# A talking-heads attention with a soft mixture of experts: a pair's first block mixed on four 64x64 tiles of TensorE, in an order of TensorE that is written out

## The chip, the cores and the metric

The kernel runs on one core of one Trainium2 chip. The metric is the device time of one execution in microseconds (us); before the change its median over 3 runs is 9190.56 us (9187.51 to 9199.91). The profile comes from one further execution, which took 9193.65 us.

## What is computed

Four sequences (batches) of 2048 tokens with 256 features pass through an attention layer and an expert layer, each with a residual and a layer norm. All data are float32. What matters here is the attention, which mixes its 16 heads twice:

```
logits = einsum('bhid,bhjd->bhij', q, k) * SCALE        # 16 heads of 16 features
logits = einsum('bhij,gh->bgij', logits, Wpre)          # heads mixed before the softmax
attn   = softmax(logits, axis=-1)
attn   = einsum('bhij,gh->bgij', attn, Wpost)           # and mixed again after it
out    = einsum('bhij,bhjd->bhid', attn, v)             # then Wout, residual, layer norm
```

The expert layer normalises the tokens and the columns of `mu`, forms slot weights from their products, and runs 16 small experts.

## The kernel before

For each of the 4 batches `qkv` projects and rotates q and k, `attention` does the above, and `moe` the expert layer. `attention` goes over 128 **pairs**. A pair `n` is two **blocks** (x = 0, 1) of 8 tokens; a block's 8 tokens times 16 heads fill the 128 partitions. The 2048 keys are taken in two halves (j = 0, 1) of 1024. For each pair:

- `raw_banks(n, c)` (L351, matmul at L366) forms q times k for all heads, 16 matmuls of 32x32 weights and 512 columns for each of c = 0, 1, into four PSUM banks (tiles `s`). Four copies, by VectorE (`V`, L529) or ScalarE (`S_`, L532), take them to the tile `raw`.
- `raw_rows(n)` (L376, L388) moves `raw` by eight DMAs of 256 KB on SyncE's queue into four tiles `rows`, one for each (j, x), with (token, head) on the partitions.
- `logits(n, j)` (L390, L406) mixes the heads with `Wpre`, again by 32x32 matmuls, into two two-bank PSUM tiles `l`, one for each x.
- `top` (L418, L421) takes the row maximum on VectorE, `expo` (L426, L430) the exponential with its sum on ScalarE, back into `rows`.
- `shares` (L436) and `weights` (L451) join the two halves of the softmax in a chain of tiny operations: VectorE, GpSimd, ScalarE, GpSimd twice, VectorE, GpSimd twice. The last one (L458) multiplies `Wpost`, laid out block-diagonally over the 8 tokens (`wblk_sb`, 128x128), with the softmax factors: tile `w`.
- `mix(n, x, j)` (L468, L478) multiplies 8 stretches of 128 keys of `rows`, as weights, with `w` as moving operand: 8 matmuls of 128x128 with 128 columns, into two PSUM banks (tiles `t`), which are copied to `aT` (keys on partitions) by VectorE and ScalarE.
- `values(grp, hf)` (L490, L498) multiplies with v: 64 matmuls of 128x32 weights and 64 columns for each pair, and every eighth pair `finish` (L516, L522) applies `Wout`.

The code of iteration n works on three pairs: `logits`, `top`, `expo` of pair n; `raw_banks` and `raw_rows` of pair n+2; `weights` and `mix` of pair n-1; and `values` of a group that is complete. `mix` in half j takes block x = j with both halves of its keys.

PSUM has eight banks: four for the two tiles `l` (pool `ps_l`), four (pool `ps_t`, tag `t`) that `raw_banks`, `mix`, `values` and `finish` take in turn, so each taking waits for what was taken four before it to be copied out. `raw` has two buffers, `rows` 10.

What sets the order: instructions that pass through `tc.keep_in_program_order` (`keep`) stay in the order of the code on their engine: the large copies, `top`, `expo` and the DMAs of `raw_rows`. All others, TensorE's matmuls among them, are placed by a scheduler as the program is built. It puts TensorE's work of a half as `logits`, `raw_banks`, `mix`, and `values` behind the `mix` of one half in two.

Of the kernel before, what the change touches and what calls it, by code (L numbers as in the profile page):

```python
# [16 lines left out]
P = 128  # L17
HEADS = 16
# [7 lines left out]
def kernel(  # L26
# [35 lines left out]
    ROWS = 10  # L62
# [3 lines left out]
    HT = NT // 2  # L66

# [25 lines left out]
    for i in range(IB):  # L93
        nc.scalar.dma_start(
            wblk_sb[i * HEADS : (i + 1) * HEADS, :, i], wpost.rearrange("(h g) -> h g", g=HEADS)
        )
    wout_sb = const.tile([P, KC, D], F32, tag="wout", name="wout_sb")
# [3 lines left out]
    mu_sb = work.tile([P, KC, ES], F32, tag="rows", name="mu_sb", bufs=ROWS)  # L101
    nc.scalar.dma_start(mu_sb, mu.rearrange("(c p) e -> p c e", p=P))
# [5 lines left out]
    ones = work.tile([P, P], F32, tag="k1", name="ones", bufs=6)  # L108
    nc.gpsimd.memset(ones, 1.0)
# [23 lines left out]

    sq = work.tile([P, KC, ES], F32, tag="rows", name="sq", bufs=ROWS)
    nc.vector.tensor_mul(sq, mu_sb, mu_sb)
    pn = ps_t.tile([P, 512], F32, tag="t", name="pn")
    for c in range(KC):
        nc.tensor.matmul(pn[:, :ES], ones, sq[:, c], start=(c == 0), stop=(c == KC - 1))
    rmu = work.tile([P, ES], F32, tag="k1", name="rmu", bufs=6)
    nc.scalar.activation(rmu, pn[:, :ES], AF.Sqrt)  # L140
    nc.vector.tensor_scalar_max(rmu, rmu, NORM_EPS)
    nc.vector.reciprocal(rmu, rmu)
    mun = const.tile([P, KC, ES], F32, tag="mun", name="mun")
    for c in range(KC):
        nc.vector.tensor_mul(mun[:, c], mu_sb[:, c], rmu)


# [13 lines left out]

    def k1(shape, name):
        return work.tile(shape, F32, tag="k1", name=name, bufs=6)
# [85 lines left out]
    def load_x(b, t, name):  # L249
        xt = work.tile([P, D], F32, tag="x", name=f"{name}_{b}_{t}", bufs=2)  # L250
        nc.sync.dma_start(xt, x[b, ts(t, P), :])
        return xt


    def qkv(b):
# [9 lines left out]
        def project(t):  # L265
            xt = load_x(b, t, "x")
# [3 lines left out]
            xT = k1([P, KC, P], f"xT_{b}_{t}")  # L270
# [49 lines left out]
    def attention(b, y, qT, kT, v):  # L320
        keep = tc.keep_in_program_order
        st = new_stats(f"a{b}")
# [4 lines left out]
        def pair_q(n):  # L327
# [4 lines left out]
            qb = k1([P, KC, 2, 4, 2, 2, 2], f"qb_{b}_{n}")  # L332
# [18 lines left out]
        def raw_banks(n, c, engs):  # L351
# [11 lines left out]
            for r in range(4):  # L363
                rows = slice(32 * r, 32 * (r + 1))
                for q in range(4):
                    nc.tensor.matmul(  # L366
# [7 lines left out]
            return [lambda r=r: engs[r](raw[:, 4 * c + r, :], prs[r]) for r in range(4)]  # L374
# [15 lines left out]
        def logits(n, j):  # L390
# [11 lines left out]
            for x in range(2):  # L402
                for h in range(2):
                    for q in range(4):
                        c = (q + 2 * x + h) % 4
                        nc.tensor.matmul(  # L406
# [29 lines left out]
        def shares(n):  # L436
# [4 lines left out]
            nc.vector.tensor_tensor(m, m2[:, :, 0:1], m2[:, :, 1:2], ALU.min)  # L441
            f = small.tile([P, 2, 2], F32, tag="f", name=f"f_{b}_{n}")
            nc.gpsimd.tensor_tensor(f, m.to_broadcast([P, 2, 2]), m2, ALU.subtract)  # L443
            nc.scalar.activation(f, f, AF.Exp)  # L444
# [6 lines left out]
        def weights(n):  # L451

            s = state[n]
            f, z = s["f"], s["z"]
            nc.vector.reciprocal(z, z)  # L455
            nc.gpsimd.tensor_tensor(f, f, z.to_broadcast([P, 2, 2]), ALU.mult)
            w = work.tile([P, 4, HEADS * IB], F32, tag="w", name=f"w_{b}_{n}", bufs=2)
            nc.gpsimd.tensor_tensor(  # L458
                w,
                wblk_sb.rearrange("p g i -> p (g i)").unsqueeze(1).to_broadcast([P, 4, HEADS * IB]),  # L460
                f.rearrange("p x j -> p (x j)").unsqueeze(2).to_broadcast([P, 4, HEADS * IB]),
                ALU.mult,
            )
            s["w"] = w
# [3 lines left out]
        def mix(n, x, j, engs):  # L468
# [6 lines left out]
            for r in range(2):  # L475
                pt = ps_t.tile([P, 4, P], F32, tag="t", name=f"t_{b}_{n}_{x}_{j}_{r}")
                for a in range(4):
                    nc.tensor.matmul(  # L478
                        pt[:, a, :], e[:, ts(4 * r + a, P)], s["w"][:, 2 * x + j, :],
                        start=True, stop=True,  # L480
                    )
                t0 = j * HT + 4 * r
                engs[r](
                    aT[grp][:, t0 : t0 + 4, :, ts(k, IB)],
                    pt.rearrange("p a (g i) -> p a g i", i=IB),
                )

        outT = {}

        def values(grp, hf):  # L490
# [4 lines left out]
            for t in range(NT):  # L495
                for c in range(4):
                    g0 = 2 * (4 * hf + c)
                    nc.tensor.matmul(  # L498
# [7 lines left out]
            if part == 0 and hf == 0:  # L506
                outT[it] = k1([P, KC, P], f"aoT_{b}_{it}")
            dst = outT[it][:, hf, ts(part, GI)]
            nc.vector.tensor_copy(dst, po[:, 0, :])  # L509
            nc.vector.copy_predicated(dst, odd, po[:, 1, :])  # L510
            if hf == 1:
                aT.pop(grp)
                if part == P // GI - 1:
                    finish(it)

        def finish(it):  # L516
            oT = outT.pop(it)
            xt = load_x(b, it, "xr")
            nc.gpsimd.tensor_add(xt, xt, bout_sb)
            pz = ps_t.tile([P, 512], F32, tag="t", name=f"pz_{b}_{it}")  # L520
            for c in range(KC):
                nc.tensor.matmul(  # L522
                    pz[:, :D], oT[:, c, :], wout_sb[:, c, :], start=(c == 0), stop=(c == KC - 1)
                )
            nc.vector.tensor_add(y[:, it, :], pz[:, :D], xt)
            norm_stats(y[:, it, :], it, st)
# [8 lines left out]
        nop = [lambda: None] * 4  # L535
        for n in range(2):
            for c in range(KC):
                for f in raw_banks(n, c, (V, S_, V, S_)):
                    f()
            raw_rows(n)  # L540
        for n in range(n_pairs + 3):
            cur, nxt, prv = n < n_pairs, n + 2 < n_pairs, 0 < n <= n_pairs

            grp, hf = divmod(n - per - 1, per)
            val = 0 <= grp < N // GI
            for j in range(2):
                if cur:
# [225 lines left out]
```

## Time and profile before

| | us |
|---|---|
| profiled execution | 9193.65 |
| its span (first to last instruction of the core) | 9191.9 |
| four attention stages (95 to 2159, 2385 to 4445, 4671 to 6742, 6969 to 9034) | 2064, 2060, 2071, 2065 |
| between and behind them (projection, experts) | 95, 226, 226, 227, 158 |
| TensorE busy with matmuls | 8249.7 |
| VectorE busy | 5541.1 |
| ScalarE busy | 4961.1 |
| GpSimd busy | 1845.8 |

In the profile PE is TensorE's matmuls, PEld its weight loads (which overlap them), DVE VectorE, ACT ScalarE, POOL GpSimd, SP SyncE. A group's line has the source line, the engine, the operation, the tile written and the tiles read, the shape and the count, then the busy time in all and the mean of one in ns. One float32 matmul of the code stands as two weight loads and two matmul records, called passes here (16384 matmuls at L478, 32768 records). A matmul's record reaches from its start to a modelled end, so records of one stream overlap, and the time that one takes of TensorE is the distance between starts.

### The profile page before, as it was taken

Reading aid. Unit: us, or ns where it says so; the run is one execution under the profiler, and the core shown is the slowest. Engines: PE = TensorE matmul, PEld = TensorE weight load, DVE = VectorE, ACT = ScalarE, POOL = GpSimd, SP = SyncE. Lnnn points to the kernel's source line nnn. Section 1 sums busy time; section 2 is a strip of 40 time slices with the busy share of each in tenths; the row PEclk is TensorE's granted clock in tenths of the full one; section 3 lists DMA queues with packets and bytes.
Section 4 is the critical chain, followed back from the end, with each engine's and each line's share of the span. In section 5 each row is a group of like instructions: output and inputs, shape, how many; then the busy total and the mean of one; then the engine's idle time right before and its main releaser. Section 6 shows DMA issues by size and latency. Waiting matters only on the chain. (4 is left out here: it accounts for less than half of the span.)

```text
span 9191.9 us, 373485 instructions
## 1 busy us (share of the span) xinstructions
PE 8249.7 (90%) x166484; PEld 6122.8 (67%) x166484; DVE 5541.1 (60%) x9074; ACT 4961.1 (54%) x9758; POOL 1845.8 (20%) x6481
## 2 busy tenths in 40 slices
PE   7999999997899999999689999999968999999996
PEld 4666776675576677676556676767755666776675
DVE  5666666665666666666466666666645666666664
ACT  3555555553455555555345555555534555555553
POOL 2221222111221122211122211221112221122211
PEclk9999999998999999999899999999989999999998
DMA  4555555552455555555145555555514555555551
GB/s 104 136 136 136 136 133 136 133 139 53 111 136 132 136 136 134 135 135 136 48 112 135 136 137 134 136 134 134 136 45 113 135 135 135 136 138 133 136 135 45
DMA packets 654551, 1140.00 MB, mean 124 GB/s; under 512 B 95760, under 2 KB 127120, under 8 KB 652944
## 3 DMA queue, kind: packets, MB, share of 16 engines
q1 hardware_dynamic: 616704, 1099.18, 49.7%
q8 instruction: 1309, 21.45, 1.0%
q10 hardware_dynamic: 36240, 16.93, 0.7%
q14 instruction: 298, 2.44, 0.1%
HBM read 33.71 MB, written 8.39 MB: 5 GB/s over the span
## 5 line engine op out<-in xcount | busy, mean ns | idle before, releaser
L478 PEld LDWEIGHTS t<-w,rows 128*128 128x128 f32 x32768 | 3760.5, 193 | 1352.9 <-ACT raw L532 753.0
L478 PE MATMUL t<-w,rows 128*128 128x128 f32 x32768 | 3945.4, 279 | 444.0 <-ACT raw L532 439.1
L421 DVE TENSOR_REDUCE m<-l 128x1 f32<-128x1024 f32 x2048 | 2497.0, 1220 | 970.2 <-PE l L406 970.2
L532 ACT COPY raw<-s 128x512 f32<-128x512 f32 x2552 | 1445.6, 590 | 2782.7 <-PE s L366 1646.9
L430 ACT ACTIVATE rows<-l,m 128x1024 f32<-128x1024 f32 x2048 | 2315.1, 1130 | 68.4 <-DVE m L421 60.8
L366 PE MATMUL s<-kT,qb 32*32 32x512 f32 x32768 | 1766.5, 606 | 72.3 <-issue 61.6
L529 DVE COPY aT<-t 128x512 f32<-128x512 f32 x2048 | 1396.6, 682 | 354.5 <-PE t L478 353.7
L532 ACT COPY aT<-t 128x512 f32<-128x512 f32 x2048 | 1219.5, 596 | 596.8 <-PE t L478 596.6
L406 PE MATMUL l<-rows,wmix_sb 32*32 32x512 f32 x32768 | 1413.8, 601 | 59.6 <-issue 35.1
L529 DVE COPY raw<-s 128x512 f32<-128x512 f32 x1544 | 1055.3, 684 | 194.6 <-PE s L366 163.3
L366 PEld LDWEIGHTS s<-kT,qb 32*32 32x32 f32 x32768 | 667.2, 103 | 738.1 <-issue 485.5
L498 PE MATMUL o<-aT,v 128*32 128x64 f32 x65536 | 1024.6, 220 | 17.8 <-issue 17.8
L498 PEld LDWEIGHTS o<-aT,v 128*32 128x32 f32 x65536 | 941.4, 110 | 80.1 <-issue 19.1
L343 POOL TENSOR_TENSOR qb<-qT,hmask 128x16 f32<-128x16 f32 (+3 forms) x3584 | 650.5, 221 | 1437.5 <-PE s L366 1437.5
L443 POOL TENSOR_TENSOR f<-m,m 128x4 f32<-128x4 f32 x512 | 102.8, 201 | 3850.3 <-DVE m L441 3850.3
L455 DVE RECIPROCAL z<-z 128x2 f32<-128x2 f32 x512 | 85.1, 166 | 860.8 <-POOL z L448 860.8
L458 POOL TENSOR_TENSOR w<-wblk_sb,f 128x512 f32<-128x512 f32 x512 | 533.5, 1042 | 40.1
L406 PEld LDWEIGHTS l<-rows,wmix_sb 32*32 32x32 f32 x32768 | 337.8, 103 | 301.6 <-issue 139.9
L509 DVE COPY aoT<-o 128x32 f32<-128x32 f32 x512 | 98.3, 192 | 673.9 <-PE o L498 673.9
L430 ACT ACTIVATION_READ_ACCUMULATOR rows<-l,m 128x1 f32 x2048 | 435.7, 213 | 0.0
L446 POOL TENSOR_TENSOR zf<-f,z 128x4 f32<-128x4 f32 x512 | 103.2, 202 | 762.1 <-ACT f L444 762.1
L301 POOL TENSOR_TENSOR s<-qk,wq 128x256 f32<-128x256 f32 x128 | 115.8, 924 | 497.4 <-DVE qk L285 484.7
(122 smaller groups left out, 2620.4 us busy)
## 6 DMA issues: line engine op xcount, KB each, us to landing
rows<-raw SPq DMA_DIRECT2D x4096, 256.0 KB
x<-in_x_dram SPq DMA_DIRECT2D x64, 128.0 KB
xr<-in_x_dram SPq DMA_DIRECT2D x64, 128.0 KB
out_dram<-qT SPq DMA_DIRECT2D x16, 512.0 KB
wm<-in_w_dram ACTq DMA_DIRECT2D x8, 512.0 KB
wm<-in_w_dram ACTq DMA_DIRECT2D x4, 1024.0 KB
wq<-in_wqkvT_dram ACTq DMA_DIRECT2D x4, 768.0 KB
wq<-in_bqkv_dram ACTq DMA_DIRECT2D x4, 384.0 KB
```

The lines of the kernel that those rows point to most:

```text
L301: nc.gpsimd.tensor_mul(s[:, :, a, :], qk[:, :, 1 - a, :], ss[a])
L343: nc.gpsimd.tensor_tensor(qb[:, :, g, s0:s1, :, :, x].rearrange("p c s i h -> p c (s i) h"), qT[:, t, :, i0:i1].unsqueeze(3).to_broadcast( ...
L366: nc.tensor.matmul(prs[r][32 * q : 32 * (q + 1), :], qb[rows, c, q % 2].rearrange("p s i h x -> p (s i h x)"), kT[rows, c, ts(q, QN)], sta ...
L406: nc.tensor.matmul(pls[x][32 * c : 32 * (c + 1), ts(h, 512)], wmix_sb[32 * q : 32 * (q + 1), :], raws[n][j][x][32 * q : 32 * (q + 1), ts(h ...
L421: nc.vector.tensor_reduce(s["m2"][:, x, j : j + 1], s["l", j][x], AX.X, ALU.max, negate=True)
L430: nc.scalar.activation(s["e", j][x], s["l", j][x], AF.Exp, bias=s["m2"][:, x, j : j + 1], accum_out=s["z2"][:, x, j : j + 1],)
L446: nc.gpsimd.tensor_tensor(zf, f, z2, ALU.mult)
L458: nc.gpsimd.tensor_tensor(w, wblk_sb.rearrange("p g i -> p (g i)").unsqueeze(1).to_broadcast([P, 4, HEADS * IB]), f.rearrange("p x j -> p ...
L478: nc.tensor.matmul(pt[:, a, :], e[:, ts(4 * r + a, P)], s["w"][:, 2 * x + j, :], start=True, stop=True,)
L498: nc.tensor.matmul(po[32 * c : 32 * (c + 1)].rearrange("p a i -> p (a i)"), v[:, t, g0 * HD : (g0 + 2) * HD], at[:, t, g0 : g0 + 2, :].rea ...
L529: keep(nc.vector.tensor_copy(dst, src))
L532: keep(nc.scalar.copy(dst, src))
```

## The change

1. TensorE's matmuls in `attention` pass through `keep`, and the loop is rewritten: `values` first, then in each half `raw_banks`, `logits`, `mix` of both blocks of pair n-1 with that half of the keys. `values` comes one iteration later (n - per - 2 in place of n - per - 1), and the copies stand in a fixed order, one of each `mix` on each engine.
2. `rows` has 12 buffers in place of 10; the tag `k1` (six buffers) is gone, its tiles take `rows` buffers or buffers of their own (`qb` three).
3. Block x = 0 is mixed by 64x64 matmuls with 64 columns. The weights `wblk_sb` are zero outside the diagonal over tokens, so partitions 0 to 63 (4 tokens) reach only the columns of these 4 tokens: `wquad_sb` (128 x 64) holds the two nonzero 64x64 parts, one above the other. Each 128 keys of `rows` take four matmuls, (row half r) x (column half c), in place of one; row half r goes to PSUM bank r. The copy to `aT` then writes runs of 4 tokens for 8 stretches of keys, in place of runs of 8 for 4.
4. The norm of `mu` moves from the start of the program into each `moe`. `finish` is called behind `logits`, and its load of x comes a half earlier.

The core of the diff:

```diff
-    ROWS = 10
+    ROWS = 12
+    IQ = IB // 2
+    wquad_sb = const.tile([P, HEADS, IQ], F32, tag="wquad", name="wquad_sb")
+    nc.vector.tensor_add(wquad_sb, wblk_sb[:, :, :IQ], wblk_sb[:, :, IQ:])
...
+        def matmul(*args, **kw):
+            keep(nc.tensor.matmul(*args, **kw))
...
-            w = work.tile([P, 4, HEADS * IB], F32, tag="w", name=f"w_{b}_{n}", bufs=2)
-            nc.gpsimd.tensor_tensor(
...
+            s["w"] = []
+            for x, blk in enumerate((wquad_sb, wblk_sb)):
+                shape = [P, 2, blk.shape[1] * blk.shape[2]]
+                w = work.tile(shape, F32, tag=f"w{x}", name=f"w{x}_{b}_{n}", bufs=2)
+                nc.gpsimd.tensor_tensor(
...
-            for r in range(2):
-                pt = ps_t.tile([P, 4, P], F32, tag="t", name=f"t_{b}_{n}_{x}_{j}_{r}")
-                for a in range(4):
-                    nc.tensor.matmul(
-                        pt[:, a, :], e[:, ts(4 * r + a, P)], s["w"][:, 2 * x + j, :],
-                        start=True, stop=True,
-                    )
...
+            if x == 0:
+                for a in range(HT):
+                    for r in range(2):
+                        for c in range(2):
+                            k0 = a * P + 64 * c
+                            matmul(
+                                pts[r][64 * c : 64 * (c + 1), ts(a, HEADS * IQ)],
+                                e[64 * r : 64 * (r + 1), k0 : k0 + 64],
+                                w[64 * r : 64 * (r + 1)],
+                                start=True, stop=True,
+                            )
+                own = [(ts(j, HT), slice(k * IB + r * IQ, k * IB + (r + 1) * IQ)) for r in range(2)]
+            else:
+                for a in range(HT):
+                    matmul(pts[a // 4][:, ts(a % 4, P)], e[:, ts(a, P)], w, start=True, stop=True)
...
-        for n in range(n_pairs + 3):
+        for n in range(n_pairs + 4):
...
-            grp, hf = divmod(n - per - 1, per)
-            val = 0 <= grp < N // GI
+            grp, hf = divmod(n - per - 2, per)
+            if 0 <= grp < N // GI:
+                values(grp, hf)
             for j in range(2):
+                raw = raw_banks(n + 2, j) if nxt else nop
                 if cur:
                     logits(n, j)
-                fs = raw_banks(n + 2, j, (S_, V, S_, V if j == 0 else S_)) if nxt else nop
                 if prv and j == 0:
                     weights(n - 1)
+                while todo:
+                    finish(todo.pop())
+                t0 = mix(n - 1, 0, j) if prv else nop
+                t1 = mix(n - 1, 1, j) if prv else nop
+                for f, eng in zip(raw, (S_, V, S_, V)):
+                    f(eng)
                 if cur:
                     top(n, j, 0)
-                fs[0]()
-                fs[1]()
+                t0[0](S_)
                 if cur:
                     expo(n, j, 0)
                     top(n, j, 1)
-                fs[2]()
-                fs[3]()
+                t0[1](V)
+                if j == 0:
+                    t1[0](S_)
                 if cur:
                     expo(n, j, 1)
-                if prv:
-                    mix(n - 1, j, 0, (V, S_))
-                    mix(n - 1, j, 1, (V, S_))
...
+                    if j == 1:
+                        shares(n)
+                if j == 1:
+                    t1[0](S_)
+                t1[1](V)
                 if j == 1:
                     if nxt:
                         raw_rows(n + 2)
-                    if val:
-                        values(grp, hf)
...
-            if cur:
-                shares(n)
```

## The prediction

> **What bounds the kernel now.** First the page: engine totals, then the costliest groups (busy us in all, mean ns of one, idle before, and who ended it).
>
> ```profile
> PE 8249.7 (90%) x166484; PEld 6122.8 (67%) x166484; DVE 5541.1 (60%) x9074; ACT 4961.1 (54%) x9758; POOL 1845.8 (20%) x6481
> ...
> L478 PE MATMUL t<-w,rows 128*128 128x128 f32 x32768 | 3945.4, 279 | 444.0 <-ACT raw L532 439.1
> ...
> L366 PE MATMUL s<-kT,qb 32*32 32x512 f32 x32768 | 1766.5, 606 | 72.3 <-issue 61.6
> ...
> L498 PE MATMUL o<-aT,v 128*32 128x64 f32 x65536 | 1024.6, 220 | 17.8 <-issue 17.8
> ```
>
> TensorE is the bound, and `mix` is nearly half of its work. Next the waits by engine (us in total, times, longest):
>
> ```profile
> ACT raw L532 <- DMA rows<-raw: 1100.5, 303, 6.5
> ...
> PE t L478 <- ACT raw L532: 439.1, 900, 1.2
> ```
>
> In some pairs the copies to `raw` wait until `raw_rows` has read the buffer, and in most halves `mix` waits about half a us for a copy to hand it a PSUM bank. The waits of SyncE's queue say why the transfers are late, namely that their `rows` buffers come free only when `mix` has read them:
>
> ```profile
> SPq L388 <- PE t L478: 4526.4, 2008, 8.1
> ```
>
> Last, the timeline of one undisturbed pair (start, length, engine, line, operation):
>
> ```profile
> 1001.11 1.22 PE L406 MATMUL l<-rows,wmix_sb 32*32 32x512 f32 x32
> 1001.99 1.49 PE L366 MATMUL s<-kT,qb 32*32 32x512 f32 x32
> ...
> 1002.30 1.23 DVE L421 TENSOR_REDUCE m<-l 128x1 f32<-128x1024 f32 x1 [1.29 <-PE l L406]
> ...
> 1003.44 0.68 DVE L529 COPY raw<-s 128x512 f32<-128x512 f32 x1
> 1003.77 1.12 ACT L430 ACTIVATE rows<-l,m 128x1024 f32<-128x1024 f32 x1
> ...
> 1003.93 3.84 PE L478 MATMUL t<-w,rows 128*128 128x128 f32 x32 [0.45 <-ACT raw L532]
> 1004.04 1.22 DVE L421 TENSOR_REDUCE m<-l 128x1 f32<-128x1024 f32 x1
> ...
> 1004.88 1.07 ACT L532 COPY raw<-s 128x512 f32<-128x512 f32 x2
> ...
> 1007.70 1.99 PE L498 MATMUL o<-aT,v 128*32 128x64 f32 x128
> ...
> 1009.76 0.19 DVE L509 COPY aoT<-o 128x32 f32<-128x32 f32 x1 [1.27 <-PE o L498]
> ...
> 1012.58 3.81 PE L478 MATMUL t<-w,rows 128*128 128x128 f32 x32 [0.54 <-ACT raw L532]
> ...
> 1016.32 1.22 PE L406 MATMUL l<-rows,wmix_sb 32*32 32x512 f32 x32
> ```
>
> The pair takes 1016.32 - 1001.11 = 15.21 us. The mean is longer: in four stretches of 1900 us inside the stages the once-a-pair operation L441 stands 119, 119, 119 and 120 times, so 7600 / 477 = **15.93 us**. Of the 0.72 between, `finish` is 0.28 (with it, `values` to `mix` takes 1045.87 - 1038.77 = 7.10 us, without it 1012.58 - 1007.70 = 4.88, once in eight pairs); the remaining 0.44 I put down to transfers.
>
> **Prices from these rows.** A full-array pass: (3.84 - 0.28) / 32 = 0.111 us from start to start. A `values` pass (64 columns, four column tiles in turn): (1.99 - 0.22) / 127 = 0.0139, so four tiles take 0.056 a round. A change of tile shape: the last L478 pass starts at 1007.49 and streams 0.11; L498 starts at 1007.70, so 0.1. `logits` with `raw_banks`: 1001.11 to 1003.48, 2.37. Step from one operation to the next on the same engine: VectorE maximum 1.14, copy 0.60; ScalarE exponential 1.11, copy 0.54. A copy starts about 0.04 to 0.07 behind the last record's end.
>
> **The change, part by part.**
>
> *Block 0 on four tiles.* Each half loses 16 of 32 full-array passes (16 x 0.111 = 1.78) and gains 64 small ones: 8 stretches x 2 passes = 16 rounds of four tiles. No row has 64x64 tiles. From below: the `values` round, 0.056 (same columns, wider weights there split in four). From above: all four one behind the other, 4 x 0.056 = 0.22. Between them lies the start spacing inside L366, some 0.017 a pass in the trace, 0.067 a round. I take 0.062, near both close rows, because L366 and L406 show 16 tiles with row and column offsets running together (32 records of 606 ns within 1.49 us). So block 0 costs 16 x 0.062 = 0.99, **0.79 less**, and one more change of shape, +0.1. The weights of a tile (64 columns) should load beside the running pass, as they do at L478 (PEld 3.65 beside 3.84 us).
>
> A rule that speaks against this: the Trainium skill, "TensorE: Matmul & The Clock Gate", section "Wait — 56ns, not 53.3ns?", says that matmul starts never come closer than about 25 ns, and 62 ns where the sequencer decodes in software. By it block 0 would cost 64 x 25 = 1.6 us (no gain to speak of) or 4.0 us (a loss); the 13.9 ns of the `values` passes is below both, so I follow the row.
>
> *The fixed order.* `raw_banks` ahead of `logits` lets the copies out of the four banks run under `logits`, which hides the 0.5 us wait per half. What it makes late instead is the way back: the next `raw_banks` needs the four banks of `mix`. I follow one half from the start of block 0 (0.00). TensorE: block 0 to 0.99, block 1 from 1.09 to 2.87, free at 2.97. ScalarE: first `t` copy at 1.25 (0.98 + 0.27), exponential 1.79, in half j = 0 then copy 2.90 to 3.49, exponential 3.44 to 4.56. VectorE: maxima at 0.10 and 1.24, copy 2.38 to 3.06, last copy 3.10 (block 1 has ended) to 3.78. So the fourth bank of `raw_banks` starts at 3.85, about 0.55 behind what TensorE could do. From there to the next block 0 is 2.37, less 0.35 for the three banks already started (L366's starts spread over 1.49 - 0.61 = 0.88 us in two passes; three quarters of one of them), plus 0.1 for the shape: 2.1. **Half j = 0: 5.95.** In half j = 1 `values` comes between: 2.97 + 1.78 + 0.1 = 4.85 for `raw_banks`; the last ScalarE copy, pinned behind both exponentials and the factor, ends at about 4.8, which is just in time; the fourth bank waits for the two small copies of `values` (5.00 to 5.45) and starts at 5.5. **Half j = 1: 7.6.** With `finish` at 0.28, a pair is 13.55 + 0.28 = **13.83 us**.
>
> What is queued behind those pinned waits: on ScalarE the exponentials wait behind the first `t` copy (counted above). The factor chain ends in VectorE's reciprocal, behind the `values` copies at 5.45, then GpSimd: 0.2 and block 0's `w`, between 0.2 (smallest GpSimd rows) and 0.5 (half of L458's 1.04): ready by 6.4, needed at 7.6. Without that 1.2 us of cover it would cost up to 0.5 a pair (250 us). GpSimd's pieces for `qb` (1.3 us a pair) run three pairs ahead and are not in the chain; GpSimd is at 20%.
>
> *Twelve `rows` buffers.* The eight issues on SyncE's queue drag over a whole pair today, 4526 us of waiting for `mix` in all. With 12 they go out when `raw` is copied, and 57% of 15.93 = 9.1 us of transfer (DMA share in the stages) has a pair's 13.8 us to land. I take the 0.44 as gone; if not, it is 0.44 x 504 = 220 us back.
>
> *The copies of block 0* write runs of 4 elements. Runs of 8 cost 682 and 596 ns, unbroken ones 684 and 590, so I take nothing; if they doubled, each half would gain 0.65 us on either engine, 655 us in all.
>
> *Moved ends.* The norm of `mu` in each `moe` costs VectorE about 1.3 us ahead of the layer norm, 5 us over four batches; its transfer and GpSimd's square lie under the 12 us of VectorE statistics there. The rest of `qkv` and `moe` only changes buffers: nothing, within 10 us either way.
>
> **The sum.** A stage of 2065 us holds 2065 / 15.93 = 129.6 periods; 126 of them are full ones, 504 in four batches. 504 x (15.93 - 13.83) = 1058 us. 9193.65 - 1058 + 5 = 8141; the median of the runs stands 3 us below the profiled execution, so **8140**.
>
> **Rivals.**
> 1. *The tiles do not load beside the passes, or two of four overlap* (chance 0.12). A round is then about 0.118 (0.11 is twice the `values` round), block 0 costs 1.89, both halves grow by 0.9: 15.63 a pair, 9194 - 504 x 0.30 = 9040. For it: 64-wide weights on 64 rows are in no row. Against: L406's 32 passes within 1.22 us.
> 2. *The fixed order turns waits into stalls* (0.18): the transfers stay late by 0.44 and the copies add up to 0.5 more, since nothing can be pulled ahead on TensorE: 14.3 to 14.9 a pair, 8380 to 8680. For it: the 1100 us of copies that wait for DMA. Against: the buffers.
> 3. *Slower: the four tiles run one at a time* (0.06). 64 passes at 0.056 are 3.57 us, 2.6 more in each half: 19.0 a pair, 9194 + 504 x 3.1 = 10750. It decides from a round of about 0.127 on, where block 0 has eaten 1.05 us per half.
> 4. *It nets out* (0.02): a round near 0.127, 9190.
>
> That the order is not what the diff says can be left out: in the built program TensorE's sequence is `raw_banks`, `logits`, 32 matmuls of 64x64, 8 of 128x128 in each half.
>
> **Numbers.** Forecast 0.62: 7800 to 8380, its low end where the bank waits vanish, which leaves TensorE's own 2 x (2.97 + 2.37) + 1.88 + 0.28 = 12.84 a pair, 7640, hardly reached. Rivals 2, 1, 3, 4 as above. The range 7800 to 8900 takes in the forecast, rival 2 and doubled block-0 copies (8800). A difference below 0.2% (18 us) is about what cannot be told from none. Faster: 0.62 + 0.18 + 0.12 = 0.92; same 0.02; slower 0.06.
>
> **What would show it.** Right: L478's successor for block 0 with 64 passes in about 1.0 us, block 1 in 1.8; copies to `raw` no longer waiting for DMA; TensorE waiting 0.3 to 0.6 us for ScalarE or VectorE ahead of a `raw_banks` bank; L441's successor some 137 times in 1900 us. Wrong: a block 0 of 1.9 or 3.6 us, copies of block 0 well over 0.7 us, `mix` waiting for GpSimd's `w`, or `logits` waiting for `rows`.

## The result and the profile after

| | before | after |
|---|---|---|
| device time, median of 4 runs each | 9190.40 us (9187.51 to 9199.91) | 9420.58 us (9412.60 to 9435.05) |
| ratio, 95% interval | | 1.025 (1.0233 to 1.0268) |
| span of the profiled execution | 9191.9 us | 9415.2 us |
| mean granted TensorE clock | 0.977 | 0.965 |

The change made the kernel 2.5% **slower**. The forecast was 8140 us, 11% faster.

The page of after, first lines, engine totals and two of the queues (packets, MB, share of the 16 DMA engines):

```profile
span 9415.2 us, 471708 instructions
...
PE 8232.6 (87%) x215648; PEld 5725.2 (61%) x215648; DVE 5925.1 (63%) x9590; ACT 4671.9 (50%) x9256; POOL 1824.5 (19%) x7000
...
q1 hardware_dynamic: 616704, 1099.18, 46.7%
q8 instruction: 1694, 27.75, 1.3%
```

TensorE is less busy than before, in a longer span. It has 215648 - 166484 = 49164 more passes, each with a weight load. Queue q1 carries the transfers that SyncE issues, the `rows` transfers above all; queue q8 brings instructions. It was 1309 packets and 21.45 MB before, so the 98328 added records took 6.30 MB: **64 bytes a record, and a packet (16 KB) holds 256 of them**. All of q8 is TensorE's: 1694 x 256 = 433664, and the trace has 433690 records of TensorE in after (passes, weight loads and some 2400 others).

The timeline of after in an undisturbed pair, TensorE alone (start, length, engine, line, operation; all matmuls now pass through the helper at L306, so they are told apart by tile and shape):

```profile
1003.75 1.49 PE L306 MATMUL s<-kT,qb 32*32 32x512 f32 x28
...
1006.68 3.14 PE L306 MATMUL t<-w,rows 64*64 64x64 f32 x80
1009.75 1.99 PE L306 MATMUL o<-aT,v 128*32 128x64 f32 x128
1011.68 1.33 PE L306 MATMUL s<-kT,qb 32*32 32x512 f32 x28
...
1014.45 3.27 PE L306 MATMUL t<-w,rows 64*64 64x64 f32 x80
1017.65 1.49 PE L306 MATMUL s<-kT,qb 32*32 32x512 f32 x28
```

From `raw_banks` to `raw_banks` this is 1017.65 - 1003.75 = 13.90 us, 1.31 less than the 15.21 of before. Both blocks of a half (64 small and 16 full passes under one entry) take 3.1 us; the 64 small ones start between 1006.68 and 1007.63, one every 15 ns, and take about 1.0 us. So the work on the tiles is what the prediction said. Yet the mean pair did not get shorter. Over the inner pairs of the four stages (eight left out at either end of each) it is 16.04 us after and 15.97 before (the once-a-pair operation is L427 in after, L441 in before). Three hundred us later in the same kernel the pair looks like this:

```profile
1300.66 0.68 PE L306 MATMUL t<-w,rows 64*64 64x64 f32 x27
1302.40 2.78 PE L306 MATMUL t<-w,rows 64*64 64x64 f32 x53 [1.06 <-issue]
...
1314.23 1.44 PE L306 MATMUL l<-rows,wmix_sb 32*32 32x512 f32 x20
1316.62 1.06 PE L306 MATMUL l<-rows,wmix_sb 32*32 32x512 f32 x7 [0.95 <-issue]
```

TensorE stops in the middle of a stream, after 27 passes of `mix` and after 20 of `logits`. No engine, no transfer of data and no bank is named as what it waits for: "issue" is time in which the profile shows no reason. The trace's DMA records show one. A 16 KB packet of q8 ran from 1299.58 to 1300.83, and TensorE resumed at 1302.40; another ran from 1314.29 to 1315.25, TensorE resumed at 1316.62. The stalls end 1.2 to 1.8 us (median 1.5) behind the end of a fetch of TensorE's own instructions.

That TensorE waits for just this packet can be counted. Number its records by their starts: packet k (the first is 0) then brings record 449 + 256k and the 255 behind it. Of the 719 gaps in after that end in this way, 652 end exactly at such a record, k being the packet that has just come, and none of the 1693 such records starts sooner than 1.15 us behind the end of its packet. The place is the same, 449, in the traces of all fifteen kernels of this document.

Counting every gap of over 0.45 us between TensorE's starts that ends in this way behind a fetch gives the accounts below. (At the records 449 + 256k alone it is a little less: 0.42 us a pair in before, 1.72 in after, 0.11 for the 0.33 of none_moved further down. The rest, 0.04 to 0.24, are other short gaps.) They are used for all experiments: the undisturbed pair, the 0.28 of `finish`, and the **fetch stalls** should add up to the mean pair.

| us a pair | undisturbed | finish | fetch stalls | sum | mean measured | fetches a pair |
|---|---|---|---|---|---|---|
| before | 15.21 | 0.28 | 0.46 | 15.95 | 15.97 | 2.52 |
| after | 13.90 | 0.28 | 1.78 | 15.96 | 16.04 | 3.27 |

In after, fetches among dense `rows` transfers (150 or more packets of q1 started in the 1.5 us ahead) cost 0.94 us each, those in quiet times 0.03. In before the two cost 0.15 and 0.20, so a dense time alone makes no stall. The traces show what does. Among dense transfers a fetch ends 3.1 us (median) behind the first record of the packet before it, in before as in after; in quiet times 1.9 and 2.1. TensorE can take it up 1.4 to 1.5 us later, 4.5 us in all for a dense one. Up to then it must live on the packet before, and in those dense times the 256 records of that packet last, the stall itself left out, 6.4 us in before but 3.8 in after.

The waits of TensorE (us in total, times, longest) show the same, somewhat low, since the modelled ends of matmuls hide part of a gap. First before:

```profile
PE s L366 <- issue: 61.6, 75, 1.4
...
PE l L406 <- issue: 35.1, 62, 1.3
```

and after, the first six rows but `PE pu`:

```profile
PE t L306 <- issue: 270.7, 263, 2.8
PE pqk L257 <- ACT xT L253: 155.9, 63, 3.2
...
PE s L306 <- issue: 121.9, 105, 2.1
PE o L306 <- issue: 121.7, 166, 5.0
PE l L306 <- issue: 119.3, 120, 1.9
```

The four "issue" rows are 634 us; the same tiles had 116 before.

So the stages are only 38 us longer in all (8088 for 8050, from the first to the last once-a-pair operation of each batch). The rest of the 223 us of span lies **between the stages**: from the last such operation of a batch to the first of the next it is 327.4, 327.0 and 323.0 us for 275.5, 283.4 and 280.3, the start 163.9 for 122.9, the end 186 for 180: 185 us together. There the `qkv` steps come every 6.5 to 8.4 us in place of 4.0, and the second line of the fence names the wait: `pqk` for `xT`, 155.9 us (32.5 before).

### The profile page after: what moved, and what is told of

Same layout as the page of the kernel before. It is cut to its first block, busy times and chain, and to the rows that moved or that the text cites. A ratio compares the mean times of both kernels' runs of the same rounds, so it can differ in the third digit from the quotient of the medians.

```text
span 9415.2 us, 471708 instructions
## 1 busy us (share of the span) xinstructions
PE 8232.6 (87%) x215648; PEld 5725.2 (61%) x215648; DVE 5925.1 (63%) x9590; ACT 4671.9 (50%) x9256; POOL 1824.5 (19%) x7000
## 3 DMA queue, kind: packets, MB, share of 16 engines
q8 instruction: 1694, 27.75, 1.3%
## 5 line engine op out<-in xcount | busy, mean ns | idle before, releaser
L306 PEld LDWEIGHTS t<-w,rows 64*64 64x64 f32 x81920 | 3040.2, 147 | 1249.1 <-issue 533.9
L306 PE MATMUL t<-w,rows 64*64 64x64 f32 x81920 | 3349.5, 235 | 298.8 <-issue 270.7
L306 PE MATMUL l<-rows,wmix_sb 32*32 32x512 f32 x32768 | 2207.3, 603 | 137.5 <-issue 119.3
L306 PE MATMUL s<-kT,qb 32*32 32x512 f32 x32768 | 2023.1, 609 | 155.5 <-issue 121.9
L538 DVE COPY raw<-s 128x512 f32<-128x512 f32 x2048 | 1366.4, 689 | 771.5 <-PE s L306 651.2
L541 ACT COPY raw<-s 128x512 f32<-128x512 f32 x2048 | 1113.9, 598 | 1143.6 <-issue 969.0
L306 PEld LDWEIGHTS l<-rows,wmix_sb 32*32 32x32 f32 x32768 | 914.6, 103 | 565.2 <-issue 272.6
L306 PE MATMUL o<-aT,v 128*32 128x64 f32 x65536 | 1070.2, 220 | 122.8 <-issue 121.7
L306 PEld LDWEIGHTS o<-aT,v 128*32 128x32 f32 x65536 | 959.8, 110 | 206.9 <-issue 145.8
L306 PEld LDWEIGHTS s<-kT,qb 32*32 32x32 f32 x32768 | 452.0, 103 | 912.5 <-issue 423.7
L257 PE MATMUL pqk<-wq,xT 128*128 128x512 f32 x256 | 181.0, 846 | 171.6 <-ACT xT L253 155.9
L447 POOL TENSOR_TENSOR w<-wblk_sb,f 128x256 f32<-128x256 f32 x512 | 314.2, 614 | 0.0
```

The lines of the kernel that those rows point to most:

```text
L257: nc.tensor.matmul(pqk[:, : 2 * D], xT[:, c, :], wqkv_sb[:, c, : 2 * D], start=(c == 0), stop=(c == KC - 1),)
L306: keep(nc.tensor.matmul(*args, **kw))
L447: nc.gpsimd.tensor_tensor(w, blk.rearrange("p g i -> p (g i)").unsqueeze(1).to_broadcast(shape), f[:, x, :].unsqueeze(2).to_broadcast(shap ...
L538: keep(nc.vector.tensor_copy(dst, src))
L541: keep(nc.scalar.copy(dst, src))
```

## The experiments

**Theory A**: TensorE waits for its own instruction fetches when these come among dense `rows` transfers. The tiles need more fetches (3.27 for 2.52), and the twelve `rows` buffers pack the transfers densely. The tiles themselves are worth what was worked out. **Rival B**: the number of instructions alone costs the time, whatever the transfers do. **Rival C**: the fixed order and its bank waits cost it. Apart from these, x and `xT` now share the `rows` buffers, which explains the time between the stages.

The runs of before beside these kernels had medians of 9181 to 9200 us; with each kernel stand its own median and, where it was timed, its ratio with the 95% interval.

### The first four: transfers halved, tiles undone, buffers as before, x apart

*half_moved*: the transfers of x = 0 only.

```diff
-            for x in range(2):
+            for x in range(1):
                 for q in range(2):
...
-                            raws[n][j][x][32 * q : 32 * (q + 1), ts(h, 512)],
+                            raws[n][j][0][32 * q : 32 * (q + 1), ts(h, 512)],
```

> Four of the eight transfers of raw_rows are left out (block 1's): both blocks' logits are made from block 0's rows, all other work is as in the changed kernel. Theory A (TensorE waits for its own instructions, whose 16 KB transfers stand behind the dense transfers of rows): the stalls in the middle of TensorE's streams fall from about 1.8 us a pair to 0.6 or less, a pair goes from 15.9 to some 14.5, the whole to 8600 to 8850. Theory B (the number of TensorE's instructions alone bounds it, 842 a pair at a fixed fetch rate): the pair stays at 15.9, the whole at 9380 to 9440. Theory C (the written order and its four PSUM banks make the waits): unchanged too, 9380 to 9440.

Measured: 9024.99 us (one execution). Stalls 1.09 us a pair, mean pair 15.30. Half as many fetches came in dense transfers (426 for 812), and those cost as much as ever (1.01 each). The direction is A's, the size is not: the stalls fell by 40%, not by two thirds.

*full_both*: everything of the change but the tiles.

```diff
-            for x, blk in enumerate((wquad_sb, wblk_sb)):
+            for x, blk in enumerate((wblk_sb, wblk_sb)):
...
-            if x == 0:
+            if x == 2:
                 for a in range(HT):
```

> Block 0 back on the full array, everything else (order, copies, twelve rows buffers) as in the changed kernel. Theory A: an undisturbed pair grows from 13.9 to 15.2 or 15.4, the fetch stalls fall from 1.8 us a pair to about 0.7 as there are 648 instructions in place of 842; so the pair stands near 16.0 and the whole at 9350 to 9550. Theory C (the order is the loss, the tiles gain in full): the whole rises by the 1.4 us a pair that the tiles save, to 10000 to 10200. Tiles that do not save at all: 9100 to 9250.

Measured: 9643.03 us (9639.48 to 9651.14), ratio 1.0508 (1.0493 to 1.0524). Undisturbed pair 15.16, mean 16.52, stalls 0.91 with the 2.52 fetches of before. So without the tiles the change is 5% slower, and the tiles as such **gain** 222 us (9643 - 9421). The fixed order did nothing for the undisturbed pair of full passes (15.16 for 15.21), and against before the same number of fetches costs twice as much (0.91 for 0.46).

*r10_split*: 10 `rows` buffers as before, and `raw_rows` in the order j, x, q.

```diff
-    ROWS = 12
+    ROWS = 10
...
-            for x in range(2):
-                for q in range(2):
-                    for j in range(2):
+            for j in range(2):
+                for x in range(2):
+                    for q in range(2):
```

> Ten rows buffers in place of twelve, and raw_rows' eight transfers in the order of the key halves, so that the last four wait until mix of the next iteration has freed their buffers: two bursts of four instead of one of eight. Theory A: shorter queues ahead of the instruction fetches, the stalls fall from 1.8 us a pair to 0.6 to 1.2, the whole to 8900 to 9250. Theory D (the twelve buffers are what the new order needs, and transfers that come late cost more than the queue): 9450 to 9800. Theory C: 9400.

Measured: 9398.68 us (9375.84 to 9421.08), ratio 1.0241 (1.0218 to 1.0263); stalls 1.58, a fetch in dense transfers 0.74. The issues are looser, nearly all in twos (1923 of 2150 runs of issues less than 1 us apart, 8 of three or four), and the stalls hardly fall. Why is seen with *spaced*, below.

*x_own*: the x tiles of `qkv` in two buffers of their own.

```diff
-            xt = load_x(b, t, k2([P, D], f"x_{b}_{t}"))
+            xt = load_x(b, t, work.tile([P, D], F32, tag="xq", name=f"x_{b}_{t}", bufs=2))
```

> The projection's x tiles in two buffers of their own again, instead of the shared rows buffers; the attention is untouched. If the shared buffers are what made a projection step 6.5 us in place of 4.0, the stretches between the attention stages shrink by 40 to 50 us each and the whole falls by 150 to 200 us, to 9220 to 9270. If the step is slower for another reason (the order that the scheduler gives ScalarE), 9400 to 9430.

Measured: 9210.52 us (9201.00 to 9238.91), ratio 1.0039 (1.0024 to 1.0054). Between the stages 278.2, 277.0 and 274.7 us, the start 115.8: 210 us are back, and the wait is that of before:

```profile
PE pqk L257 <- ACT xT L253: 31.3, 62, 0.5
```

The pairs did not change (16.05, stalls 1.75). This is the loss between the stages, shown. All later kernels contain this edit or one like it; *before_small*, made from before, needs none.

### Transfers taken away, and a first try at spacing them

*none_moved*: no `rows` transfer at all; `logits` reads `raw` where it lies (`raw` has three buffers, `rows` eight).

```diff
-                            raws[n][j][x][32 * q : 32 * (q + 1), ts(h, 512)],
+                            raws[n]["from"][32 * q : 32 * (q + 1), 4 * j + 2 * x + h, :],
...
-                        keep(nc.sync.dma_start(raws[n][j][x][:, ts(q, QN)], raw[p0 + x : p0 + 32 : 2]))
+                        pass
```

> All eight transfers of raw_rows are left out: logits reads the tile raw as it lies (raw has three buffers, rows eight), all other work stays; x has its own buffers. Theory A (the instruction fetches stand behind the transfers): hardly a stall is left in TensorE's streams, below 0.15 us a pair, the pair 14.1 to 14.4, the whole 8300 to 8450. Theory B (the number of instructions): the stalls of 1.75 us a pair stay, the whole 9150 to 9250.

Measured: 8322.53 us (one execution), mean pair 14.30, half of the pairs 13.77, stalls 0.33. The page:

```profile
span 8320.8 us, 462966 instructions
...
PE 7874.3 (95%) x215648; PEld 5618.9 (68%) x215648; DVE 5899.4 (71%) x9590; ACT 4661.7 (56%) x9256; POOL 1831.4 (22%) x7000
...
q8 instruction: 1692, 27.72, 1.4%
```

The same passes as in after, all but two of its 1694 fetches, and 1.4 us a pair less stalling. **B falls here**: the instructions are all there. C falls with it, as the order of TensorE is the same too.

*paced*: two transfers at a time, each pair of them behind a 4-byte transfer that reads a row maximum and so waits for it.

```diff
+            if part and n - 1 in state:
+                g = small.tile([1, 1], F32, tag="gate", name=f"gate_{b}_{n}_{part}")
+                gj, gx = GATES[part]
+                keep(nc.sync.dma_start(g, state[n - 1]["m2"][0:1, gx, gj : gj + 1]))
```

> x has its own buffers, and raw_rows' eight transfers go out two at a time: two at once, then two behind each of three row maxima of the next iteration (a transfer of one number that reads the maximum holds SyncE's queue until then). Theory A with the length of the queue: a fetch finds at most two or three transfers ahead, the stalls fall from 1.75 to 0.5 to 0.9 us a pair, the whole to 8750 to 8900. Theory A without it (any running transfer delays a fetch as much): 9150 to 9250. Lateness: if the last two transfers hold back the next copies to raw, 9300 or more.

Measured: 9235.02 us (9225.47 to 9241.16), ratio 1.0046 (1.0029 to 1.0063), stalls 1.62. A miss. In part the kernel did not do what it was made for: in 1500 us, 59 times four transfers in a row still went out less than 1 us apart; in x_own four or more did 74 times. Most of the others left in twos, as in r10_split, and that was no help either.

*small_dma*: each transfer in two of 64 partitions.

```diff
-                        keep(nc.sync.dma_start(raws[n][j][x][:, ts(q, QN)], raw[p0 + x : p0 + 32 : 2]))
+                        for u in range(2):
+                            keep(nc.sync.dma_start(raws[n][j][x][64 * u : 64 * (u + 1), ts(q, QN)], raw[p0 + x + 16 * u : p0 + 16 * (u + 1) : 2]))
```

> x has its own buffers, and each transfer of raw_rows is cut into two of 64 partitions, 16 a pair with the same bytes. If a fetch takes turns with whole transfers on a DMA engine, its wait halves: 8750 to 8900. If it stands behind all that was handed out before, nothing changes: 9150 to 9250. If SyncE's issue (0.55 us each, 16 a pair) becomes late: 9300 or more.

Measured: **8648.10 us** (8643.79 to 8652.41), ratio 0.9407 (0.9389 to 0.9426), mean pair 14.80, stalls 0.65 with the same 3.27 fetches. It beats both the kernel before and the change.

*tiles_x*: x_own with both blocks on 64x64 tiles.

```diff
-            for x, blk in enumerate((wquad_sb, wblk_sb)):
+            for x, blk in enumerate((wquad_sb, wquad_sb)):
...
-            if x == 0:
+            if x < 2:
                 for a in range(HT):
```

> x has its own buffers, and both blocks of a pair are mixed on 64x64 tiles. By TensorE's work alone a pair falls by another 1.4 us, to 8500. Theory A: TensorE reads 1034 instructions a pair in place of 842 in less time, so the stalls grow from 1.75 to about 2.7 us a pair and eat most of the gain: 8950 to 9300.

Measured: 10290.83 us, ratio 1.1194 (1.1172 to 1.1217): stalls 4.46 a pair with 4.02 fetches. A had expected far less. Part of it is the clock: inside the stages the records show half of full clock for 1567 us, 61 in before, 150 in after.

### Why cutting a transfer in two helps, and where tiles stop paying

The diffs of *small_full* and *small_tiles* are those of full_both and tiles_x on top of small_dma (small_full's x tiles use two buffers of a tag that `moe` has as well); that of *before_small* is small_dma's, on the kernel before.

> The kernel of small_dma (x tiles of the qkv stage in two buffers of their own, each rows transfer cut in two of 64 partitions), but with block 0 on the full array like block 1. It says what the 64x64 tiles are worth once the waits for instruction fetches are small. Theory A (TensorE waits for its own instruction fetches when they stand among dense rows transfers; work on tiles is worth what it was on undisturbed pairs): the undisturbed pair is that of full_both, 15.1 to 15.2 us against 13.8 in small_dma; with the finish of rows and stalls of 0.3 to 0.6 a pair the mean is 15.5 to 15.9, so 504 x 0.7 to 1.1 = 350 to 550 us over small_dma's 8648: 9000 to 9200. Rival (the gain of small_dma came from the transfers alone, and tiles with their added instructions net out): within 100 us of small_dma, 8550 to 8750.

Measured: 9117.22 us (9114.66 to 9119.78), ratio 0.9901 (0.9868 to 0.9934). Undisturbed pair 15.16, stalls 0.35, mean 15.72. So the tiles of block 0 are worth 9117 - 8648 = 469 us, where the fetches are let through; 222 where they are not. As A had it.

> The kernel of small_dma with both blocks of a pair on 64x64 tiles. tiles_x, the same with whole transfers, had 4.02 fetches and 4.46 us of stalls a pair, 10291 us. Theory A with stalls that come from a fetch standing behind a whole transfer: stalls of 0.3 us a fetch at most, 1 to 1.3 us a pair, on an undisturbed pair 0.8 us shorter than small_dma's, 13.0: a mean of 14.2 to 14.6, so 8350 to 8550. Rival (with four fetches a pair the fetching itself can't keep up, however the transfers are cut): stalls of over 2.5 us a pair, over 9000.

Measured: 9655.98 us (9647.85 to 9664.12), ratio 1.0486 (1.0446 to 1.0526): stalls 3.80. The rival of this run was right. Here the stalls do not need dense transfers: of the fetches with 20 to 100 packets of q1 started in the 1.5 us ahead 90% are followed by a stall, of those with 100 to 150 56%, of those with fewer than 20 79%. The timeline of small_tiles, TensorE:

```profile
1306.12 2.10 PE L306 MATMUL t<-w,rows 64*64 64x64 f32 x128
1308.14 0.98 PE L306 MATMUL o<-aT,v 128*32 128x64 f32 x53
1310.43 1.31 PE L306 MATMUL o<-aT,v 128*32 128x64 f32 x75 [1.32 <-issue]
```

128 passes of 64x64 with their weight loads are 256 records, a whole packet, and TensorE is through them in 2.0 us; `values` behind them has 256 in 2.0 us as well. A fetch takes 1.1 us and the restart 1.4 more, 2.5 us. My estimate from these rows: with both blocks on tiles, TensorE uses up a packet faster than the next is fetched and taken up, for 4 us on end, once a pair. With block 1 on the full array (32 records in 1.8 us) there is a rest between the two. Over the inner pairs (medians, nearly all fetches being in the times called quiet above): the next packet is in 2.5 us behind the first record of the one before and can be taken up at 3.9, which lasts 3.3 us in small_tiles; in small_dma it is in at 2.2, can be taken up at 3.7, and the packet before lasts 4.3. The waits for the `values` passes fit: in small_tiles

```profile
PEld o L306 <- issue: 844.7, 508, 4.2
```

that is nearly every pair, while with block 1 on the full array it is 69.0 us in 76 times in small_dma, and in *spaced* (below)

```profile
PEld o L306 <- issue: 64.7, 141, 4.4
```

*col_dma* cuts each transfer by columns, so that each piece is on all 128 partitions:

```diff
+                        for u in range(2):
+                            m = slice(u * QN // 2, (u + 1) * QN // 2)
+                            keep(nc.sync.dma_start(raws[n][j][x][:, ts(q, QN)][:, m], raw[p0 + x : p0 + 32 : 2, :, m]))
```

> x_own with each rows transfer cut in two by columns, not by partitions: 16 transfers a pair as in small_dma, of the same bytes each, but each on all 128 partitions and with descriptors of 512 B in place of 1 KB. It tells the two readings of small_dma apart. A1 (a fetch waits because one whole transfer occupies all DMA engines at once; 64 partitions leave half of them free): landings show 16 updates per transfer as in x_own, stalls stay at 1.4 to 1.8 us a pair, 9100 to 9300. A2 (twice as many issues on SyncE spread the traffic evenly over the pair): stalls fall as in small_dma to about 0.65 a pair, 8600 to 8750.

Measured: 8703.49 us (8696.89 to 8710.09), ratio 0.9452 (0.9417 to 0.9487), stalls 0.67. The range is A2's: a piece need not be on 64 partitions to help. (Its packets are of 1 KB and those of x_own of 2 KB, twice what the expectation has.) That does not yet say that small_dma helps in the same way. At 694 of the 1694 fetches of x_own 14 or more packets of q1 were in flight, in small_dma at 5, and its packets of 2 KB take 84 ns (median) for 133. So A1, by which the pieces leave some DMA engines free, may still hold for small_dma; the runs do not separate it from the spacing.

> The kernel before, with nothing changed but that each rows transfer is cut in two of 64 partitions. It says what the size of transfers is worth without the change. Theory A: before lost 0.46 us a pair in stalls at the end of instruction fetches, and most of them go: a mean pair of 15.6 to 15.75 for 15.97, so 110 to 190 us less, 8990 to 9080. Rival (the gain belongs to the fixed order and the bigger pool, before has its transfers spread already): within 40 us of before, 9150 to 9230; or slower, if SyncE's 16 issues a pair delay the rows.

Measured: 9208.86 us (9187.98 to 9225.77), ratio 1.001 (0.9998 to 1.0022), stalls 0.58. The rival of this run was right: before has nothing to gain from it. There SyncE waited for `mix` 2008 times for 4096 transfers and in the whole run issued more than three less than 1 us apart only 9 times. Its transfers were more loosely spaced than those of after, though nobody had planned it.

*spaced* has whole transfers, each followed by one of 4 bytes that waits for nothing:

```diff
                         keep(nc.sync.dma_start(raws[n][j][x][:, ts(q, QN)], raw[p0 + x : p0 + 32 : 2]))
+                        g = small.tile([1, 1], F32, tag="gate", name=f"gate_{b}_{n}_{x}_{q}_{j}", bufs=8)
+                        keep(nc.sync.dma_start(g, eps_sb[0:1, 0:1]))
```

> x_own with whole rows transfers (128 partitions, 256 KB, eight a pair), each followed on SyncE's queue by a transfer of 4 bytes that waits for nothing: 16 issues a pair as in small_dma and col_dma, but the moved pieces as large as in x_own. It tells size from spacing. Size reading (a fetch stands behind whole transfers of 256 KB; 128 KB pieces are what helped): stalls stay at 1.4 to 1.8 us a pair, 9100 to 9300. Spacing reading (SyncE's issues of 0.6 to 0.9 us, twice as many, keep the transfers from piling up, about half as many packets in flight around a fetch): stalls of 0.6 to 1.0 a pair, 8650 to 8850.

Measured: **8655.31 us** (8654.45 to 8656.18), ratio 0.9425 (0.9398 to 0.9453), stalls 0.72, mean pair 14.90. The same bytes in the same 256 KB pieces, and eight transfers a pair that move nothing of use take 555 us off x_own. SyncE's queue in spaced (each issue takes 0.6 us):

```profile
1302.39 0.61 SPq L374 DMA_DIRECT2D rows<-raw  x1
1303.04 0.61 SPq L376 DMA_DIRECT2D gate<-eps_sb  x1
1303.75 0.60 SPq L374 DMA_DIRECT2D rows<-raw  x1
1304.40 0.61 SPq L376 DMA_DIRECT2D gate<-eps_sb  x1
```

`rows` transfers leave every 1.3 us. In after they mostly leave 0.6 to 1.2 us apart (median 0.88), and the packets of one take 1.06 us (median) from the first start to the last, so they pile up.

The pile can be read from the traces, as a whole `rows` transfer is 144 packets of q1 and the order of the packets tells which are whose. The first packet starts 0.66 us behind the end of the issue where nothing stands ahead. The median is 0.74 in spaced, 0.77 in col_dma and 0.76 in before, but 1.54 in after, 1.53 in x_own, 1.61 in full_both, and 1.41 and 1.39 in r10_split and paced. Over 1 us are none in spaced, 47% in before, 83% in after. In r10_split and paced, then, transfers that leave in twos still stand in line, which fits that these two did not help. The pieces of small_dma (72 packets) stand in line as well, 1.42 us, and it helps all the same.

The fetches of after and x_own are late as well. For 575 packets of the inner pairs TensorE waited in x_own, and their fetches started 2.1 us (median) behind the first record of the packet before. The same 575 packets, of the same instructions, were fetched from 1.5 us on in spaced and from 1.1 us on in small_dma, and TensorE waited for 51% and 32% of them; in paced it was 2.2 us and 78%. TensorE's rows of spaced:

```profile
PE t L306 <- issue: 52.2, 112, 1.4
PE s L306 <- issue: 44.7, 68, 1.6
PE o L306 <- issue: 37.4, 71, 4.2
...
PE l L306 <- issue: 27.9, 60, 0.8
```

162 us in all, for 634 in after. The accounts of the kernels that settle it:

| us a pair | undisturbed | finish | fetch stalls | sum | mean measured | time |
|---|---|---|---|---|---|---|
| full_both | 15.16 | 0.28 | 0.91 | 16.35 | 16.52 | 9643 |
| small_full | 15.16 | 0.28 | 0.35 | 15.79 | 15.72 | 9117 |
| after | 13.90 | 0.28 | 1.78 | 15.96 | 16.04 | 9421 |
| spaced | 13.77 | 0.28 | 0.72 | 14.77 | 14.90 | 8655 |
| small_dma | 13.80 | 0.28 | 0.65 | 14.73 | 14.80 | 8648 |
| none_moved | 13.77 | 0.28 | 0.33 | 14.38 | 14.30 | 8323 |

**What stays open.** The fetch itself is no longer among dense transfers (1.12 us) than in quiet ones (1.11); it is its start that is late, as the same packets in three kernels show. The trace has no moment at which a fetch was asked for, so where it stands until then, in line behind packets of `rows` or elsewhere, is inferred and not seen. Nor was it tried whether the 4-byte transfers help by the time of their issue alone, or also by standing between the others. What helps in small_dma, where the pieces do stand in line but fewer are in flight, is open too.

## Why the prediction was wrong, point by point

**The step that failed is the account of the 0.72 us between the undisturbed and the mean pair.** The prediction has "the remaining 0.44 I put down to transfers" and then "I take the 0.44 as gone", since twelve buffers would let the transfers go early. The 0.44 were TensorE's fetch stalls, 0.46 measured in before. The sum had no term for instructions at all: neither for the 192 added records a pair nor for what an "issue" wait is. That row stood in the prediction's first fence (`72.3 <-issue 61.6`) and was read over. The term measured 1.78 us a pair: 1.32 more than in before, where the forecast had 0.44 less. That is 504 x 1.76 = 890 us of the 1280 by which the forecast missed.

**"The rest of `qkv` and `moe` only changes buffers: nothing, within 10 us either way"** failed too. It cost 185 us between the stages, and x_own got 210 back with one tag. A shared pool is a wait: whoever takes a buffer waits for the reader of the one before it, and `xT` came late to TensorE by it. Together the two make 890 + 185 = 1075 us; what is left of the miss, some 200 us, is in the undisturbed pair, two points below, and in the sum's rounding.

**Block 0 on four tiles: right.** 0.99 worked out, and 1.09 with the change of shape; 1.09 measured from the first small pass to the first full one (median of 1024 halves), with 15 ns from start to start. Here the Trainium skill, "TensorE: Matmul & The Clock Gate", section "Wait — 56ns, not 53.3ns?", was weighed, with its 25 ns between starts; the trace is below that, and the measurement decides. The gain on TensorE was right as well: 15.16 - 13.80 = 1.36 us an undisturbed pair between small_full and small_dma, where the prediction had 2 x (0.79 - 0.1) = 1.38. Of this 0.30 went to the stalls of the added fetches even there (0.65 for 0.35).

**The order hides the bank waits: right, but it gains little.** No gap is left ahead of `mix`. From block 0 to block 0, as in the working, half j = 1 takes 1014.45 - 1006.68 = 7.77 where 7.6 was worked out, and half j = 0 the rest of the 13.90, 6.13 for 5.95. `raw_banks` with `logits`, where the last passes of `raw_banks` slip among those of `logits` as they wait for the fourth bank, had 5.95 - 2.97 = 2.98 and 7.6 - 4.85 = 2.75 in the sum and take 2.93 and 2.77: right. Too low was the full pass. Those of block 1 start every 118 ns, not 111, so block 1 with the change of shape behind it takes 1.98 (median of 1024 halves) for 1.88, which is 0.20 a pair. Without the finish the pair is 13.90, not 13.55, and 504 x 0.35 = 176 us is most of the 200 left above. On full passes the same order gains 0.05 (15.16 for 15.21), where the sum had 15.21 - 13.55 - 1.38 = 0.28 for it.

**The buffers: right in what they do, wrong in what follows.** Copies to `raw` no longer wait for transfers (92 us for 1100), just as "what would show it" had it; SyncE waits for the copies now and not for `mix`:

```profile
SPq L374 <- DVE raw L538: 4251.5, 508, 30.6
...
SPq L374 <- PE t L306: 142.3, 389, 0.8
```

But this wait for `mix` had spaced the transfers out. Without it they came in bursts: in full_both, which has the new order and buffers and the passes of before, a transfer's first packet starts 1.61 us behind its issue, for 0.76 in before, and the stalls are 0.91 for 0.46 at the same number of fetches. Which part of that comes from the buffers and which from the order was not run apart.

**Copies in runs of 4: right**, 687 and 587 ns for 682 and 596 over the copies of both blocks; no form of them stands out (at most 694 and 594 in 99 of 100). **The weights for block 0 in time: right**, its passes wait 9 us for GpSimd in all. (GpSimd's pieces for `qb` are 46.6 us in the 500 us of the prediction's window, 1.5 us a pair and not 1.3; nothing rests on it.)

**The rivals.** Rival 1 (tiles two of four) and 3 (one at a time) did not happen. Rival 2 was near in form, waits turned into stalls of a fixed order, but it sought them in transfers and copies and priced them at up to 1.1 us a pair, under the gain (its two parts, 0.44 and 0.5, make 14.8, not the 14.9 it ends at). The slower case rested on a mechanism (slow tiles) that the trace already spoke against; the one that came, instruction supply, was in none of the cases.

## What to carry to other kernels

Where a change adds many small instructions to the engine that is the bound, count them in bytes (here 64 a record, 16 KB a fetch) and read the "issue" waits: they are a term of the sum, and it grows with the density of the data transfers beside them. A wait that is taken off a DMA queue can have been what spaced its transfers; look at what a burst will collide with, and if need be space the issues at the rate at which they land. Splitting a matmul into small tiles pays as long as the engine does not, packet after packet, run through its instructions faster than the next come (with both blocks on tiles a packet lasted 3.3 us and the next could be taken up at 3.9): one block of two gained 469 us, both lost 1008 against that.

## What the runs showed of the hardware

- TensorE's instruction fetches come in 16 KB packets of 256 records and 1.1 us. TensorE resumes a median of 1.4 to 1.5 us behind the end of one that it waited for, and in after never took one up sooner than 1.15 us.
- Four 64x64 float32 tiles take 64 passes of 64 columns in 1.0 us, one start every 15 ns.
- An issue on SyncE's queue takes 0.6 us, so eight 4-byte transfers a pair are a way to pace it.
- Where TensorE stalls much, its granted clock is lower too: inside the stages the records show half of full clock for 1567 us in tiles_x (4.46 us of stalls a pair), 150 in after (1.78), 61 in before (0.46) and 1.6 in spaced (0.72). The mean of tiles_x is 0.907, for 0.965 in after. That the stalls are the cause was not tried.
